# A fused two-layer decoder: norms without an aggregate instruction, a feed gate by silu, and rounding and a maximum moved to ScalarE

## The chip, the cores and the metric

The kernel runs on one core of a Trainium2 chip. A core has five engines with an instruction queue each: TensorE (PE, matrix products), VectorE (DVE), ScalarE (ACT, activation functions), GpSimd (POOL), and SyncE (SP), which here only issues DMA transfers. Each engine works through its queue in order, and semaphores make one wait for another. The metric is the device time of one execution in microseconds, the median of several.

## What is computed

The reference sends 64 sequences of 128 tokens with 128 features through two layers. After each of the six blocks x becomes layernorm(x + block(x)). The blocks of layer 0 are an attention by running exp(k)-weighted means, a cross-attention with 16 heads over 77 context rows with bias and mask, and a feed of two shared and eight routed experts, two for each token. Those of layer 1 are a selective state-space scan (256 channels, 16 states), a cross-attention with 16 heads of 64 that ends in a norm of its own, and a quantised feed.

```python
def _layernorm(x, axis=-1, eps=1e-05):
    m = jnp.mean(x, axis=axis, keepdims=True)
    v = jnp.var(x, axis=axis, keepdims=True)
    return (x - m) / jnp.sqrt(v + eps)
...
    gate = jax.nn.silu(_bitlinear(x, w_gate))
    up = _bitlinear(x, w_up)
    return _bitlinear(gate * up, w_down)
```

In the scan block delta = softplus(dt @ W + bias); the state is h = exp(delta * A) * h + (delta * u) * B per step, and y = sum over the states of h * C. In the quantised feed the activations are rounded to 127 steps of each row's largest magnitude and the weights to -1, 0 and 1.

## The kernel before

Everything stays on the core between blocks, except that x of each group goes through DRAM (`mid`) and that rows are sorted by expert in DRAM (`rows_in`, `rows_out`). The 64 sequences are cut into 16 groups of 4 (128 partitions of tokens, 4 x 128 features). In layer 0 a group passes a (attention), b (cross-attention) and c (routing, shared experts); each two groups make a chunk `ch`, whose tokens are sent by indirect DMA from GpSimd (L977) into 15 tiles of 256 rows (`c_tile`, L317 to L390), multiplied by the tile's expert and gathered again (`c_get`, L392 to L426). Four chunks are done beside layer 0 and four beside layer 1. In layer 1 a group passes the scan (`scan_inputs`, `spread`, `decays`, `states`, `outputs`), cross-attention and feed.

The order of the work is made when the kernel is built. Each block is a generator that yields steps: an engine, a cost written by hand in microseconds, a key, the keys it waits for, a function that issues its instructions, and buffers from fixed lists of slots. `Flow.run` picks again and again the step that can start first by these costs, so the cost of a step, the table that it names (`exp`, `silu`, `ln`; a change of table counts 1.3) and the flag `port` (steps of VectorE and GpSimd with it are not laid over each other) decide where its instructions stand in each engine's queue. On the chip, the queues are fixed and waits are by semaphore.

The steps that the change and the prediction name:

- `norm` (L255 to L279): for each of 4 sequences VectorE takes statistics (bn_stats, L261: a row is split in two halves, each giving count, mean and summed squared deviation) and joins them (bn_aggr, L262); GpSimd adds epsilon, takes the power -0.5 and the shift (L269 to L272); ScalarE applies both (L278). It is called 16 times each for lnA, lnB and lnC (after the three blocks of layer 0), and ln1, ln2, ln3 and ln4 in layer 1; 8 of the lnC calls lie in layer 1.
- The scan: 16 pairs of states per group. Per pair VectorE makes bu = du * B (L1375) and the scan h (L1383); ScalarE the decays dA (L1359, three buffers, table `exp`); GpSimd h * C (L1407); TensorE adds up over states (L1420). The product h * C also waits for the bu of the following pair, which is issued ahead of the following scan.
- Softplus of delta (L1268 to L1299): abs on ScalarE (L1278), maximum with 0 on VectorE (L1282), then exponential and logarithm on ScalarE.
- The feed (L1702 to L1808): for each of 4 sequences TensorE makes gate and up, ScalarE tanh (L1758, same table as exp), VectorE the gate product g = (tanh + 1) * gate (L1762), times up (L1766), the row's maximum and four or five small scales (L1772, L1696 to L1699, L1774), the first half of rounding by adding a large number (L1777); ScalarE takes the number off again (L1783).
- In `c_get`, GpSimd issues two gathers per sequence (L417) and VectorE adds each, weighted, to v (L406, two instructions per sequence).
- Mask addition of cross-attention in layer 0 on GpSimd (L684), with three bias buffers and one mask buffer.

```python
            (got,) = yield S.flow.pool(2.0, k + ("got", b), out, get, S.got, landing=3.0)
            got.until = k + ("mix", b)
            yield Fork(mix(b, got))
```

Of the kernel before, what the change touches and what calls it, by code (L numbers as in the profile page):

```python
# [11 lines left out]
AF = mybir.ActivationFunctionType  # L12
ALU = mybir.AluOpType
# [4 lines left out]
P = 128  # L18
B = 64
G = 4  # L20
NG = B // G
W = G * P
M = 77
# [3 lines left out]
MAGIC = 12582912.0  # L27
RMS_EPS = 1.1920929e-07
LN_EPS = 1e-5
# [39 lines left out]
class Flow:  # L69
# [18 lines left out]
    pe, act, dve, pool = _maker("PE"), _maker("ACT"), _maker("DVE"), _maker("POOL")  # L88
# [92 lines left out]
def decoder(ctx: ExitStack, tc: tile.TileContext, t: dict, out: bass.AP):  # L181
# [30 lines left out]
    pool.memset(mhalf, -0.5)  # L212
    mmagic = new(const, [P, 1], "mmagic")
    pool.memset(mmagic, -MAGIC)
    before = new(const, [P, NE, NE], "before")
    pool.memset(before, 1.0)
    pool.affine_select(
# [37 lines left out]
    def norm(flow, pn, key, o, v, deps):  # L255

        kind = key[0]
        mv, st = new(pn, [P, G, 2], kind + "mv"), new(pn, [P, G, 6], kind + "st")

        def stats(b):  # L260
            dve.bn_stats(st[:, b, :], v[:, b, :])  # L261
            dve.bn_aggr(mv[:, b, :], st[:, b, :])  # L262

        for b in range(G):
            yield flow.dve(0.55, key + ("st", b), deps, lambda: stats(b))
        r, sh = new(pn, [P, G], kind + "r"), new(pn, [P, G], kind + "sh")

        def steps():
            pool.tensor_scalar(r, mv[:, :, 1], LN_EPS, None, ALU.add)  # L269
            pool.tensor_scalar(sh, mv[:, :, 0], -1.0, None, ALU.mult)  # L270
            pool.tensor_tensor(r, r, mhalf[:, :G], ALU.pow)
            pool.tensor_tensor(sh, sh, r, ALU.mult)  # L272

        yield flow.pool(2.0, key + ("r",), [key + ("st", b) for b in range(G)], steps)
        for b in range(G):
            yield flow.act(
                0.5, key + (b,), [key + ("r",)],
                lambda: act(o[:, b, :], v[:, b, :], AF.Identity, bias=sh[:, b : b + 1], scale=r[:, b : b + 1]),  # L278
            )  # L279
# [112 lines left out]
    def c_get(g, S):  # L392

        k, ch = ("c", g), g // CH
        out = [("tile", ch, i, "out") for i in range(NT)]
        yield Wait(out + [("sum", g)])
        (vs,) = yield S.flow.sp(k + ("v",), [("sum", g)], lambda o: nc.sync.dma_start(out=o, in_=mid[g]), S.v)
        vs.until = ("out0", g)
        v = vs.tile

        def mix(b, got):
            j = g % CH * G + b

            def add():
                for i in range(2):
                    dve.scalar_tensor_tensor(  # L406
                        v[:, b, :], got.tile[:, i, :], gate[:, ch, i, j : j + 1], v[:, b, :], ALU.mult, ALU.add
                    )

            yield S.flow.dve(0.7, k + ("mix", b), [k + ("got", b), k + ("v",)], add)  # L410

        for b in range(G):

            def get(o):
                j = g % CH * G + b
                for i in range(2):
                    pool.indirect_dma_start(  # L417
                        out=o[:, i, :], out_offset=None, in_=rows_out[ch],
                        in_offset=bass.IndirectOffsetOnAxis(ap=pos[:, ch, i, j : j + 1], axis=0),
                    )  # L420

            (got,) = yield S.flow.pool(2.0, k + ("got", b), out, get, S.got, landing=3.0)
            got.until = k + ("mix", b)
            yield Fork(mix(b, got))
        yield from norm(S.flow, S.pn, ("lnC", g), v, v, [k + ("mix", b) for b in range(G)])
        yield S.flow.sp(("out0", g), normed(("lnC", g)), lambda: nc.sync.dma_start(out=mid[g], in_=v))  # L426

# [13 lines left out]
    with (  # L441
# [17 lines left out]
        sl_wkv = slots(4, p, [P, 2, P], "wkv")  # L459
        sl_den = slots(3, p, [P, P], "den")  # L460
        sl_y = slots(3, p, [P, G, P], "y")
        sl_ah = slots(1, p, [P, W], "ah")
        sl_v = slots(3, p, [P, G, P], "v")
        sl_bias = slots(3, p, [P, G, M], "bias")
        sl_mask = slots(1, p, [P, G, M], "mask")
        sl_cg = slots(3, p, [P, G * M], "cg")
        sl_xb = slots(2, p, [P, G, P], "xb")
        sl_qT = slots(3, p, [P, W], "qT")
        sl_kb = slots(2, p, [P, G, 4, M], "kb")
        sl_s = slots(4, p, [P, NH, M], "s")  # L470
# [5 lines left out]
        sl_eh = slots(2, p, [P, 2, W], "eh")  # L476
        sl_sum = slots(2, p, [P, G, P], "sum")
        sl_pick = slots(2, p, [P, 2, NE, CH * G], "pick")
        S = Experts(flow=flow, bank=bank, pn=pn, a=sl_a, ahead=-0.5, pace=lambda ch, i: [], **tile_slots(p, 2, 2, 2, 2, 2, 1, 3))
        zero = new(p, [P, P], "zero")  # L480
        pool.memset(zero, 0.0)

# [15 lines left out]
        scale = 8**-0.5  # L498
# [470 lines left out]
        def c_send(ch):  # L969
            yield Wait([("rank", ch), ("fill", ch)])  # L970
            for g, b, i in (key[1:] for key in sent(ch)):

                def send():
                    j = g % CH * G + b
                    if len(filled[ch]) > 1:
                        pool.memset(tick, 0.0)
                    one = pool.indirect_dma_start(  # L977
                        out=rows_in[ch], in_=CX[g, "x"][:, b, :], in_offset=None,
                        out_offset=bass.IndirectOffsetOnAxis(ap=pos[:, ch, i, j : j + 1], axis=0),
                    )  # L980
# [8 lines left out]
                yield POOL(1.0, ("send", g, b, i), [("rank", ch), ("fill", ch), ("c", g, "x")], send, landing=3.0)  # L989

        def c_shared(g):
            k = ("c", g)
# [80 lines left out]
    with (  # L1073
# [131 lines left out]
        def scan_inputs(g):  # L1205
# [61 lines left out]
            for c in range(2):  # L1267
                step = lambda z, *_: mm(  # L1268
                    z, dt_proj[:, c * P : (c + 1) * P], proj.tile[0:NS, :], start=True, stop=True
                )  # L1270
                if c == 0:
                    pz, e, delta, du = yield PE(0.95, k + ("dt", c), [k + ("proj",)], step, bank, sl_h, sl_delta, sl_du)
                else:
                    (pz,) = yield PE(0.95, k + ("dt", c), [], step, bank)
                pz.until = k + ("max", c)
                bias = dt_bias[:, c : c + 1]
                yield ACT(
                    0.7, k + ("abs", c), [k + ("dt", c)], lambda: act(e.tile[:, c, :], pz.tile, AF.Abs, bias=bias)  # L1278
                )
# [422 lines left out]
        def feed(g):  # L1702
# [6 lines left out]
            def quantise():  # L1709
                dve.tensor_reduce(am, x, AX.X, ALU.max, apply_absolute_value=True)  # L1710
                xs, xi = scales(am, G)
                dve.tensor_scalar(sg, xi, wmean[:, 0:1], 0.5, ALU.mult, ALU.mult)
                dve.tensor_scalar(su, xi, wmean[:, 1:2], None, ALU.mult)
                dve.tensor_tensor(su, su, sg, ALU.mult)
                q["xs"] = xs

            yield DVE(2.0, k + ("am",), normed(("ln3", g)), quantise)
# [26 lines left out]
            for b in range(G):  # L1744

                def gate_up(pg, pu, _):
# [29 lines left out]
                def scaled():  # L1776
                    dve.tensor_scalar(h, h, w["hs"], MAGIC, ALU.mult, ALU.add)  # L1777
# [152 lines left out]
```

## Time and profile before

| what | value |
|---|---|
| median of 3 executions | 3314.45 us (3307.13 to 3314.62) |
| the profiled execution: its time, its span | 3323.51 us, 3321.7 us |
| instructions | 55836 |
| TensorE matmul busy | 2867.3 us, 86% of the span |
| VectorE busy | 2616.4 us, 79% |
| ScalarE busy | 2097.9 us, 63% |
| GpSimd busy | 1741.2 us, 52% |
| mean granted TensorE clock | 0.941 |
| first, last scan (L1383) on VectorE | about 1117, 3187 us from the start |

The span runs from the first to the last instruction; the execution's time has 1.8 us more around it. A group of the profile is a line, an engine, an operation and its tiles, then busy time and mean nanoseconds of one, then the idle time just before these instructions and what ended it. "A <- B" in the list of waits says that A's engine stood idle until B was done. The list counts an engine's idle time, which is not the same as time lost at the end; for that there is the chain that ended last, which is followed back from the last instruction and here reaches over the last 1001 us. An operation of VectorE can last longer than its own work when GpSimd works at the same time: of the weighted sums L406 the shortest is 253 ns, the median 351, the longest 5274.

### The profile page before, as it was taken

Reading aid. Unit: us, or ns where it says so; the run is one execution under the profiler, and the core shown is the slowest. Engines: PE = TensorE matmul, PEld = TensorE weight load, DVE = VectorE, ACT = ScalarE, POOL = GpSimd, SP = SyncE. Lnnn points to the kernel's source line nnn. Section 1 sums busy time; section 2 is a strip of 40 time slices with the busy share of each in tenths; the row PEclk is TensorE's granted clock in tenths of the full one; section 3 lists DMA queues with packets and bytes.
Section 4 is the critical chain, followed back from the end, with each engine's and each line's share of the span. In section 5 each row is a group of like instructions: output and inputs, shape, how many; then the busy total and the mean of one; then the engine's idle time right before and its main releaser. Section 6 shows DMA issues by size and latency. Waiting matters only on the chain. (4 is left out here: it accounts for less than half of the span.)

```text
span 3321.7 us, 55836 instructions
## 1 busy us (share of the span) xinstructions
PE 2867.3 (86%) x19880; PEld 1937.7 (58%) x19880; DVE 2616.4 (79%) x5007; ACT 2097.9 (63%) x3831; POOL 1741.2 (52%) x1603
## 2 busy tenths in 40 slices
PE   3989999999996679889898988888899988888883
PEld 2667777776864346556464655555665655656462
DVE  3777787888754488878987888888888898879864
ACT  1655767667731566767666766666677767767653
POOL 3454564655454356445745556664645556554531
PEclk7899999999998899999998999999999999999986
DMA  5134252333223464365545554464536533333400
GB/s 152 46 95 123 71 142 71 108 105 85 67 82 117 140 232 151 128 189 172 188 149 179 178 180 166 147 213 154 173 118 196 173 119 127 116 121 122 154 23 7
DMA packets 256542, 438.23 MB, mean 132 GB/s; under 512 B 40683, under 2 KB 155014, under 8 KB 256262
## 3 DMA queue, kind: packets, MB, share of 16 engines
q1 hardware_dynamic: 248070, 417.86, 39.9%
q0 software_dynamic: 8192, 16.79, 1.6%
q8 instruction: 157, 2.57, 0.3%
q14 instruction: 123, 1.01, 0.1%
HBM read 376.37 MB, written 58.20 MB: 131 GB/s over the span
## 5 line engine op out<-in xcount | busy, mean ns | idle before, releaser
L1407 POOL TENSOR_TENSOR h<-h,C 128x1024 f32<-128x1024 f32 x256 | 604.6, 2363 | 571.4 <-DVE bu L1375 365.5
L1420 PE MATMUL acc<-h,ident 128*128 128x512 f32 x1024 | 540.1, 653 | 138.5 <-POOL h L1407 137.5
L1383 DVE TENSOR_TENSOR_SCAN h<-dA,bu 128x1024 f32<-128x1024 f32 x256 | 583.8, 2280 | 26.7 <-PE acc L1420 7.7
L1375 DVE TENSOR_TENSOR bu<-du,B 128x1024 f32<-128x1024 f32 x256 | 355.8, 1390 | 79.2 <-DMA B<-rows 77.2
L1420 PEld LDWEIGHTS acc<-h,ident 128*128 128x128 f32 x1024 | 187.2, 201 | 346.5 <-POOL h L1407 193.5
L1359 ACT ACTIVATE dA<-delta,negA 128x508 f32<-128x508 f32 x512 | 336.4, 714 | 57.2 <-DVE h L1383 56.7
L349 PE MATMUL mm<-t_rT,t_we 128*128 128x256 f32 x960 | 250.8, 394 | 14.9 <-DMA t_we<-in_we 6.7
L1609 POOL TENSOR_TENSOR s<-s,rs 128x1232 f32<-128x1232 f32 x64 | 145.6, 2276 | 175.7 <-DVE rs L1603 111.6
L349 PEld LDWEIGHTS mm<-t_rT,t_we 128*128 128x128 f32 x960 | 175.9, 194 | 76.5 <-issue 22.6
L785 POOL TENSOR_TENSOR s<-s,mx 128x1232 f32<-128x1232 f32 x64 | 144.0, 2255 | 143.9 <-DVE mx L782 69.5
L1509 PE MATMUL mm<-xT,w_yWq 128*128 128x256 f32 x512 | 165.6, 406 | 21.4 <-ACT kT L1502 8.9
L1627 ACT COPY pT<-mm 77x512 f32<-77x512 f32 x256 | 136.4, 583 | 55.9 <-PE mm L1616 53.9
L1498 ACT ACTIVATE qT<-mm,w_ybq 128x256 f32<-128x256 f32 x256 | 122.4, 478 | 68.7 <-PE mm L1510 67.8
L793 ACT COPY pT<-mm 77x512 f32<-77x512 f32 x256 | 132.7, 586 | 50.8 <-PE mm L800 45.1
L1566 PEld LDWEIGHTS mm<-kT,qT 64*128 64x128 f32 x2048 | 130.3, 194 | 51.3 <-issue 18.6
L1616 PE MATMUL mm<-ident,s 128*77 128x128 f32 x1024 | 140.9, 283 | 19.7 <-POOL s L1609 10.6
L977 POOL DMA_INDIRECT rows_in<-cx,pos x128 | 124.3, 971 | 57.9 <-DVE pos L957 24.9
L800 PE MATMUL mm<-ident,s 128*77 128x128 f32 x1024 | 139.3, 290 | 17.1 <-ACT s L787 12.4
L417 POOL DMA_INDIRECT t_got<-rows_out,pos x128 | 131.2, 1025 | 40.6 <-issue 28.5
L1616 PEld LDWEIGHTS mm<-ident,s 128*77 128x77 f32 x1024 | 118.9, 152 | 54.8 <-POOL s L1609 21.8
L1566 PE MATMUL mm<-kT,qT 64*128 64x77 f32 x2048 | 148.0, 286 | 0.9 <-DVE s L1592 0.4
L374 PEld LDWEIGHTS mm<-t_we,t_th 128*128 128x128 f32 x960 | 123.6, 197 | 32.8 <-issue 15.1
(335 smaller groups left out, 7025.5 us busy)
## 6 DMA issues: line engine op xcount, KB each, us to landing
B<-rows SPq DMA_DIRECT2D x256, 512.0 KB, 4.9
C<-rows SPq DMA_DIRECT2D x256, 512.0 KB, 4.0
t_we<-in_we SPq DMA_DIRECT2D x120, 384.0 KB, 3.6
rows_in<-zero SPq DMA_DIRECT2D x8, 1920.0 KB
t_row<-rows_in SPq DMA_DIRECT2D x120, 128.0 KB, 3.2
rows_out<-t_yo SPq DMA_DIRECT2D x120, 128.0 KB, 3.6
cg<-in_ctxT SPq DMA_DIRECT2D x32, 154.0 KB, 4.4
x<-in_x SPq DMA_DIRECT2D x16, 256.0 KB, 4.2
```

The source lines that it names most:

```text
L349: mm(o[:, c * TR : (c + 1) * TR], we.tile[:, n * 256 + c * P : n * 256 + (c + 1) * P], rT.tile, start=True, stop=True,)
L785: lambda: pool.tensor_tensor(s, s, mx.tile.unsqueeze(2).to_broadcast([P, NH, M]), ALU.subtract), port=True,
L800: nc.tensor.transpose(pt[0:M, i * P : (i + 1) * P], s[:, 4 * q + i, :], ident)
L1359: act(dA[:, j, :, 1:], delta[:, c, :, 1:], AF.Exp, scale=negA[:, c, n + j : n + j + 1])
L1375: order[g, c, n] = dve.tensor_tensor(bu, du[:, c, :].unsqueeze(1).to_broadcast([P, 2, W]), BC["B", g, c, n], ALU.mult)
L1383: dve.tensor_tensor_scan(h.rearrange("p n s -> p (n s)"), DA[g, c, n].rearrange("p n b s -> p (n b s)"), bu.tile.rearrange("p n s -> p (n ...
L1407: one = pool.tensor_tensor(h, h, BC["C", g, c, n], ALU.mult)
L1420: mm(acc, ident, HS[g, c, n][:, j, :], start=n + j == 0, stop=n + j == NS - 1)
L1509: mm(pk[:, 0 : 2 * P], yWq[:, cs], xT.tile[:, pair * 2 * P : (pair + 1) * 2 * P], start=True, stop=True)
L1566: mm(sc[:, i * M : (i + 1) * M], qT[r, i, b2 * P : (b2 + 1) * P], kT[r, i, b2 * M : (b2 + 1) * M], start=True, stop=True,)
L1609: lambda: pool.tensor_tensor(s, s, rs.tile.unsqueeze(2).to_broadcast([P, NH, M]), ALU.mult), port=True,
L1616: nc.tensor.transpose(pt[0:M, i * P : (i + 1) * P], s[:, 4 * q + i, :], ident)
```

## The change

Seven edits:

1. `norm` drops bn_aggr. GpSimd joins the two halves itself: d is the difference of the means, r the sum of the squared deviations over 128 plus epsilon plus d squared over 4, sh minus half the sum of the means. Ten instructions of GpSimd where there were four.
2. In the feed, ScalarE's silu (table `silu`) takes the place of tanh and VectorE's gate product; one small multiplication of scales goes too.
3. The first half of rounding moves from VectorE to ScalarE (scale and a bias tile `magic`).
4. Delta's maximum with 0 moves from VectorE to ScalarE (Relu with the same bias).
5. The weighted sum of an even sequence waits for the gathers of the odd one behind it as well.
6. Gathers and sends carry the flag `port`.
7. Slots in layer 0: `ah` 1 to 2, `bias` 3 to 2, `xb` 2 to 3, and the expert tiles' row buffer 2 to 1.

```diff
+    magic = new(const, [P, 1], "magic")
+    pool.memset(magic, MAGIC)
...
-        def stats(b):
-            dve.bn_stats(st[:, b, :], v[:, b, :])
-            dve.bn_aggr(mv[:, b, :], st[:, b, :])
...
-            yield flow.dve(0.55, key + ("st", b), deps, lambda: stats(b))
+            yield flow.dve(0.3, key + ("st", b), deps, lambda: dve.bn_stats(st[:, b, :], v[:, b, :]))
...
-            pool.tensor_scalar(r, mv[:, :, 1], LN_EPS, None, ALU.add)
-            pool.tensor_scalar(sh, mv[:, :, 0], -1.0, None, ALU.mult)
+            pool.tensor_tensor(d, st[:, :, 1], st[:, :, 4], ALU.subtract)
+            pool.tensor_tensor(r, st[:, :, 2], st[:, :, 5], ALU.add)
+            pool.tensor_tensor(sh, st[:, :, 1], st[:, :, 4], ALU.add)
+            pool.tensor_tensor(d, d, d, ALU.mult)
+            pool.tensor_scalar(r, r, 1.0 / P, LN_EPS, ALU.mult, ALU.add)
+            pool.tensor_scalar(d, d, 0.25, None, ALU.mult)
+            pool.tensor_scalar(sh, sh, -0.5, None, ALU.mult)
+            pool.tensor_tensor(r, r, d, ALU.add)
             pool.tensor_tensor(r, r, mhalf[:, :G], ALU.pow)
             pool.tensor_tensor(sh, sh, r, ALU.mult)
-        yield flow.pool(2.0, key + ("r",), [key + ("st", b) for b in range(G)], steps)
+        yield flow.pool(3.3, key + ("r",), [key + ("st", b) for b in range(G)], steps)
...
-            yield S.flow.dve(0.7, k + ("mix", b), [k + ("got", b), k + ("v",)], add)
+            yield S.flow.dve(0.7, k + ("mix", b), [k + ("got", b | 1), k + ("v",)], add)
...
-            (got,) = yield S.flow.pool(2.0, k + ("got", b), out, get, S.got, landing=3.0)
+            (got,) = yield S.flow.pool(2.0, k + ("got", b), out, get, S.got, landing=3.0, port=True)
...
-        sl_ah = slots(1, p, [P, W], "ah")
+        sl_ah = slots(2, p, [P, W], "ah")
-        sl_bias = slots(3, p, [P, G, M], "bias")
+        sl_bias = slots(2, p, [P, G, M], "bias")
-        sl_xb = slots(2, p, [P, G, P], "xb")
+        sl_xb = slots(3, p, [P, G, P], "xb")
...
-        S = Experts(flow=flow, bank=bank, pn=pn, a=sl_a, ahead=-0.5, pace=lambda ch, i: [], **tile_slots(p, 2, 2, 2, 2, 2, 1, 3))
+        S = Experts(flow=flow, bank=bank, pn=pn, a=sl_a, ahead=-0.5, pace=lambda ch, i: [], **tile_slots(p, 2, 1, 2, 2, 2, 1, 3))
...
-                yield DVE(
-                    0.75, k + ("max", c), [k + ("dt", c), k + ("abs", c)],
-                    lambda: dve.tensor_scalar(delta.tile[:, c, :], pz.tile, bias, 0.0, ALU.add, ALU.max),
+                yield ACT(
+                    0.7, k + ("max", c), [], lambda: act(delta.tile[:, c, :], pz.tile, AF.Relu, bias=bias)
                 )
...
-                    0.7, k + ("tanh", b), [k + ("up", b)],
-                    lambda: act(h, pg.tile, AF.Tanh, scale=sg[:, b : b + 1]), table="exp",
+                    0.7, k + ("g", b), [k + ("up", b)],
+                    lambda: act(h, pg.tile, AF.Silu, scale=sg[:, b : b + 1]), table="silu",
                 )
                 yield DVE(
-                    0.7, k + ("g", b), [k + ("tanh", b)],
-                    lambda: dve.scalar_tensor_tensor(h, h, 1.0, pg.tile, ALU.add, ALU.mult),
-                )
-                yield DVE(
-                    0.75, k + ("h", b), [],
+                    0.75, k + ("h", b), [k + ("g", b)],
                     lambda: dve.scalar_tensor_tensor(h, pu.tile, su[:, b : b + 1], h, ALU.mult, ALU.mult),
...
-                yield DVE(0.45, k + ("scaled", b), [], scaled, port=True)
+                yield ACT(
+                    0.75, k + ("scaled", b), [k + ("scale", b)],
+                    lambda: act(h, h, AF.Identity, scale=w["hs"], bias=magic),
+                )
```

The send of L989 carries the flag like the gather. In the built order, the counts per engine are the same on TensorE and SyncE; VectorE has 624 fewer instructions, GpSimd 673 more, ScalarE 96 more and 26 more table loads.

More of the change, by code (lines that the diff above doesn't have):

```diff
@@ L257, in norm @@
         kind = key[0]
-        mv, st = new(pn, [P, G, 2], kind + "mv"), new(pn, [P, G, 6], kind + "st")
-        def stats(b):
-            dve.bn_stats(st[:, b, :], v[:, b, :])
-            dve.bn_aggr(mv[:, b, :], st[:, b, :])
+        st = new(pn, [P, G, 6], kind + "st")
         for b in range(G):
-            yield flow.dve(0.55, key + ("st", b), deps, lambda: stats(b))
-        r, sh = new(pn, [P, G], kind + "r"), new(pn, [P, G], kind + "sh")
+            yield flow.dve(0.3, key + ("st", b), deps, lambda: dve.bn_stats(st[:, b, :], v[:, b, :]))
+        r, sh, d = new(pn, [P, G], kind + "r"), new(pn, [P, G], kind + "sh"), new(pn, [P, G], kind + "d")
         def steps():
-            pool.tensor_scalar(r, mv[:, :, 1], LN_EPS, None, ALU.add)
-            pool.tensor_scalar(sh, mv[:, :, 0], -1.0, None, ALU.mult)
+            pool.tensor_tensor(d, st[:, :, 1], st[:, :, 4], ALU.subtract)
[6 more added lines that the diff above has]
+            pool.tensor_tensor(r, r, d, ALU.add)
             pool.tensor_tensor(r, r, mhalf[:, :G], ALU.pow)
             pool.tensor_tensor(sh, sh, r, ALU.mult)
-        yield flow.pool(2.0, key + ("r",), [key + ("st", b) for b in range(G)], steps)
+        yield flow.pool(3.3, key + ("r",), [key + ("st", b) for b in range(G)], steps)
         for b in range(G):
@@ L987, in send @@
                     filled[ch].append(one)
-                yield POOL(1.0, ("send", g, b, i), [("rank", ch), ("fill", ch), ("c", g, "x")], send, landing=3.0)
+                yield POOL(1.0, ("send", g, b, i), [("rank", ch), ("fill", ch), ("c", g, "x")], send, landing=3.0, port=True)
         def c_shared(g):
@@ L1711, in quantise @@
                 xs, xi = scales(am, G)
-                dve.tensor_scalar(sg, xi, wmean[:, 0:1], 0.5, ALU.mult, ALU.mult)
+                dve.tensor_scalar(sg, xi, wmean[:, 0:1], None, ALU.mult)
                 dve.tensor_scalar(su, xi, wmean[:, 1:2], None, ALU.mult)
-                dve.tensor_tensor(su, su, sg, ALU.mult)
                 q["xs"] = xs
@@ L1774, in scale @@
                     dve.tensor_scalar(w["hi"], w["hi"], wmean[:, 2:3], None, ALU.mult)
-                def scaled():
-                    dve.tensor_scalar(h, h, w["hs"], MAGIC, ALU.mult, ALU.add)
                 yield DVE(1.2, k + ("scale", b), [], scale)
-                yield DVE(0.45, k + ("scaled", b), [], scaled, port=True)
+                yield ACT(
+                    0.75, k + ("scaled", b), [k + ("scale", b)],
+                    lambda: act(h, h, AF.Identity, scale=w["hs"], bias=magic),
+                )
                 (hb,) = yield ACT(
```

## The prediction

> **What bounds the kernel now.** I read the page's engine shares first, then busy time cut into stages, then the waits, then the chain that ended last. The shares of the page are means over a program with two halves, so the stages come before any of them is believed. Columns: microseconds, then busy time with instruction counts of TensorE matmul, TensorE weight load, VectorE, ScalarE and GpSimd, granted clock, DMA share, GB/s.
>
> ```profile
> 0.00:200.00 200.00, 134.38 (x1038) 91.25 (x1038) 127.27 (x379) 81.16 (x170) 77.45 (x135) 0.85 0.35 100
> 200.00:1000.00 800.00, 765.43 (x7419) 584.76 (x7417) 616.49 (x1628) 518.35 (x1017) 433.64 (x598) 0.98 0.34 95
> 1000.00:1117.00 117.00, 79.75 (x321) 46.26 (x321) 44.45 (x131) 33.36 (x48) 44.25 (x75) 0.84 0.30 99
> 1117.00:3187.00 2070.00, 1808.66 (x10477) 1156.99 (x10478) 1759.22 (x2660) 1401.58 (x2471) 1156.52 (x758) 0.95 0.49 160
> 3187.00:3321.70 134.70, 79.11 (x630) 58.44 (x628) 68.92 (x210) 63.44 (x127) 29.33 (x39) 0.76 0.02 5
> ```
>
> Row two is layer 0 in full flow: TensorE is busy 765/800 = 96%, VectorE 77%. TensorE bounds it, and VectorE work taken out there gives nothing. Row four is layer 1 with its scans, 62% of the span: TensorE 87%, VectorE 85%, ScalarE 68%, GpSimd 56%. No engine is full; two in-order queues near 86% wait for each other. Which waits:
>
> ```profile
> POOL h L1407 <- DVE bu L1375: 365.5, 110, 13.6
> PEld acc L1420 <- POOL h L1407: 193.5, 142, 7.0
> PEld acc L1420 <- issue: 148.9, 545, 0.8
> PE acc L1420 <- POOL h L1407: 137.5, 107, 6.2
> ```
>
> The largest wait of TensorE, 137.5 of about 261 idle us in row four, is for the product h*C on GpSimd, and that product waits 365.5 us for the next bu in VectorE's queue. So what stands ahead of a bu in VectorE's queue sets when TensorE gets its accumulation. The chain agrees:
>
> ```profile
> PE 13%; DVE 9%; POOL 3%; ACT 2%; issue 2%; DMA 1%; SPq 0%; POOLq 0%; DVEq 0%; ACTq 0%
> L1383 DVE TENSOR_TENSOR_SCAN h<-dA,bu 128x1024 f32<-128x1024 f32 x256 | 583.8, 2280 | 26.7 <-PE acc L1420 7.7
> L1375 DVE TENSOR_TENSOR bu<-du,B 128x1024 f32<-128x1024 f32 x256 | 355.8, 1390 | 79.2 <-DMA B<-rows 77.2
> L1359 ACT ACTIVATE dA<-delta,negA 128x508 f32<-128x508 f32 x512 | 336.4, 714 | 57.2 <-DVE h L1383 56.7
> ```
>
> The chain reaches back over the last 1001 us only; of those TensorE has 416, VectorE 312, GpSimd 107, ScalarE 74. The scan's idle time names no ScalarE decay, and the decays wait 56.7 us for scans instead: ScalarE runs ahead.
>
> **VectorE, what goes.** Durations of the trace, where visible as distance from start to start. Aggregates: statistics plus aggregate take 0.40 us, four short L1722 operations in a row 0.21 each, so 0.19 per aggregate (at least the 0.10 between an aggregate and its successor). In row four lie 260 of the 448: 49 us; 160 lie in layer 0 (30 us, behind a full TensorE), 28 in the tail. Gate product L1762: 0.79 us, 56 in row four, 44 us. Rounding L1777: 0.41 between, 56, 23 us. Delta's maximum L1282: 0.67, 30, 20 us; its wait for ScalarE (21.5 us in this stage) goes too, but what was behind it is next, so I count none. Small scales: 14 at 0.2, 3 us. Sum 139 of 1759 us.
>
> **ScalarE, what comes.** Silu takes the place of tanh at the same length (L1758, 683 ns). Maximum: like its neighbour abs L1278, 685 ns, 32 times, 22 us. Rounding with a scale and a bias: like L1783, 720 ns, 64 times, 46 us. Both may be up to 0.1 us longer or shorter each, 10 us. Table loads: the built order of the changed kernel has 172 in layer 1 against 142, and 44 against 48 in layer 0. A load takes 1283 ns in the trace: 30 x 1.283 = 38 us, together 106 us. Here the Trainium skill speaks against the change: "ScalarE: Activation LUTs", section What ACT_TABLE_LOAD costs, adds a drain of about 1.38 us to the 1283 ns, 2.66 us per switch. By that the loads would be 80 us, the sum 148. The trace shows at one of them:
>
> ```profile
> 2105.14 0.58 ACT L1258 COPY fh<-mm 48x512 f32<-48x512 f32 x1 [2.06 <-PE mm L1253]
> 2105.73 1.28 ACT L1599 ACT_TABLE_LOAD   x1
> 2107.03 1.23 ACT L1599 ACTIVATE s<-s 128x1232 f32<-128x1232 f32 x1
> ```
>
> Copy, load and exponential follow without a gap, so no drain is paid and I take 106 (1402 to about 1500 of row four, 75% of a shortened stage). 34 of the loads stand before the feed's silu and 47, six more, before decays: silu and exp now alternate within the feed. A decay behind such a pair is 2.6 us later. What hides it is the decays' lead over the scans; without the lead, a scan, the bu behind it and TensorE's accumulation wait.
>
> **GpSimd, what comes.** A norm gets eight short steps where it had two, and keeps power and product. Neighbours of the same size: L531 and L532, 0.20 us, L533 0.23, spaced 0.28 to 0.31. Six more at 0.20 to 0.29: 1.2 to 1.75 us, I take 1.6. 72 norms in layer 1: 115 us; 112 in all: 180 us. Row four rises from 56% to about 62%. The skill's "GPSIMD Engine Reference", section Engine selection, would keep elementwise work on VectorE as about twice as fast; at 128x4 the rows say 0.20 to 0.23 against 0.15 to 0.23 on VectorE (L1696 to L1714), because nearly all is fixed cost. By the rule the steps would cost VectorE half, by the rows as much. What the change buys is not speed but another queue: a norm is later by 1.6 - 4 x 0.19 = 0.8 us. Behind it in GpSimd's queue stand h*C and the softmax products L1609; they idle 747 us in all, so most of it is covered. Uncovered, the 65 norms of row four by 1.6 us: 104 us.
>
> **Pairs of transfers, slots, order.** The sums L406 take 253 ns at least, but 82.3/128 = 643 on average: 50 us are stretched beside GpSimd operations (5.7 us for two of them while h*C and softmax products ran). In the built order the two blocks of a pair follow each other, so a sum waits for one transfer more (up to 32 pairs x 2 x 0.97 us of issuing = 62 us, with a scan or an attention step behind it) or escapes some stretch and the 9.6 us of waiting seen (up to -60). I take zero: both gathers are usually issued together. The new port flags only shift order. In layer 0 the second tile row buffer goes: a row lands in 3.2 us while 60 tiles spread over some 700 us, one per 11; between 0 and +10 us, I take zero, as TensorE is full there. The opening stall stays: GpSimd's second mask addition waits 33 us for a mask queued behind two zero fills, and in the built order it still does. The tail keeps its length: per block VectorE gives up 0.79 + 0.41, ScalarE adds 0.72, two norms add 0.8 each: about -2 + 2.
>
> **The sum.** From below: a microsecond of work counts as far as its engine's work is on the chain. Cut to the chain's last 1001 us, busy time is 813 us on VectorE, 657 on ScalarE, 506 on GpSimd; so 312/813 = 0.38, 74/657 = 0.11, 107/506 = 0.21. Gain 139 x 0.38 = 53; costs 100 x 0.11 = 11 (row four's part of the 106) and 104 x 0.21 = 22; net -20 us. From above: if TensorE came as close to full in row four as in row two (96%), 1809/0.957 = 1890, -180 us. The first is too low, as it leaves out that with VectorE at 79% two queues no longer catch on each other; the second too high, as 149 us of TensorE's gaps are issue gaps at the accumulation that no VectorE time fills. Between these I take TensorE at 90%: 1809/0.90 = 2010, -60 us. The choice of 90 is mine: a third of the way, since TensorE's row two level needed VectorE at 77%, and VectorE here comes to 1620/2010 = 81%. The profiled execution took 3323.5 us (span 3321.7 and 1.8 around it), 9 above the median; less 60 it is 3263.5, and against the median 3314.5 - 60 = 3255 us.
>
> **Rivals.** *Layer 1 fills as layer 0 does*: row two shows that this program's mix can keep TensorE at 96%. Against it speak the accumulation's issue gaps. -100 to -180, some 3180 us. *TensorE holds the end anyway*: its chain share is the largest, no matmul is removed, and the -20 of the marginal sum melts with the uncovered costs: 3304 to 3324. *ScalarE becomes the bound, slower*: place, the decays behind the feed's silu in row four. All 106 us of ScalarE's added time surface if ScalarE's lead of three decay buffers is gone, against the 60 gained: +46, 3360; with a third of the gain left, up to 3380. It decides from about 60 us of the 106 on. For it: 75% in an in-order queue that also empties five PSUM banks. Against it: scans waiting for no decay, and ScalarE's 7% of the chain. *The change doesn't relieve VectorE*: excluded, 139 us are gone from its queue; only what follows is open.
>
> **How the numbers follow.** Partial relief, 3255, own range 3200 to 3304: 0.53. Full relief below 3200: 0.17. No change, within 0.3% (about 10 us, what a measurement of this kernel can tell from no change): 0.09. Slower: 0.21, of it half below 3340. The range 3165 to 3340 leaves out about 0.06 below and 0.10 above. Faster by over 0.3%: 0.70; within: 0.09; slower: 0.21.
>
> **What would show it.** VectorE's busy time down by about 170 us in all, ScalarE's up by about 100, GpSimd's by 130 to 180. Accumulation's wait for h*C (137.5) and h*C's for bu (365.5) shrink, TensorE's share between first and last scan is 90%, and layer 0's full stage stays near 96%. The slower rival shows as scans idle before ScalarE decays. I am wrong if VectorE's freed time comes back as waits for norms, table loads or banks.

## The result, and the profile after

| | before | after |
|---|---|---|
| median of four executions | 3311.89 us (3307.13 to 3314.62) | 3394.22 us (3387.50 to 3411.86) |
| ratio, 95% interval | | 1.0254 [1.0227, 1.0282] |
| profiled execution: time, span | 3323.51, 3321.7 | 3387.50, 3385.5 |
| VectorE, ScalarE, GpSimd busy | 2616.4, 2097.9, 1741.2 | 2478.6, 2203.2, 1867.8 |
| start of first scan; first to last scan start; from there to the end | 1119; 2056; 146 | 1111; 2125; 150 |

The changed kernel is slower by 82 us; 3255 was forecast, 60 faster. A second set of runs of it gave 1.0246 [1.0206, 1.0286]. The profiled spans differ by 64 us: -8 before the first scan, +68 in the scan stage, +3 behind it. So nearly all lies in the stage that the change was to shorten. The last scan of the kernel before starts at 3175 us; the 3187 given further up, where its row four ends, is 12 us later.

Busy time cut into the same five stages, after (columns as in the prediction):

```profile
0.00:200.00 200.00, 136.19 (x1096) 91.15 (x1096) 136.67 (x399) 83.67 (x174) 90.84 (x183) 0.91 0.35 101
200.00:1000.00 800.00, 757.03 (x7387) 575.31 (x7388) 599.32 (x1486) 513.18 (x1011) 470.48 (x804) 0.99 0.34 95
1000.00:1111.00 111.00, 76.02 (x293) 44.49 (x292) 34.08 (x93) 35.70 (x52) 36.49 (x62) 0.81 0.31 102
1111.00:3238.00 2127.00, 1821.34 (x10491) 1170.49 (x10510) 1651.62 (x2240) 1496.33 (x2578) 1226.44 (x1136) 0.94 0.47 155
3238.00:3385.50 147.50, 79.43 (x594) 57.97 (x596) 56.96 (x169) 74.29 (x140) 43.55 (x94) 0.75 0.02 6
```

Counted in both from the first to the last scan's start, VectorE gave up 106 us (1755 to 1649), and its idle time rose by 174 (301 to 475). TensorE works 22 us longer there (1797 to 1819) and stands idle 46 us longer (259 to 305); its share fell from 87% to 86%. No engine became full: the busiest is still TensorE, and ScalarE and GpSimd stand at 70% and 58%. The waits of the whole run:

```profile
POOL h L1410 <- DVE bu L1378: 359.4, 114, 10.5
PEld acc L1423 <- POOL h L1410: 207.9, 144, 7.7
PE acc L1423 <- POOL h L1410: 152.5, 111, 7.5
PEld acc L1423 <- issue: 149.1, 542, 0.8
```

The wait for bu is where it was (365.5 to 359.4), although VectorE has 106 us less to do in that stage: the queue in front of bu didn't get emptier in a way that reaches the accumulation. TensorE's wait for h*C rose from 137.5 to 152.5, and within the stage its wait for the other products on GpSimd, those of the softmax, rose as well (before, then after):

```profile
PE mm L1616 <- POOL s L1609: 10.6, 9, 3.7
PE mm L1619 <- POOL s L1612: 26.5, 12, 11.9
```

These two make 31 of TensorE's 46 us of added idle time. The chain that ended last, and the three groups that the prediction showed of before:

```profile
PE 36%; DVE 18%; POOL 11%; DMA 7%; ACT 6%; issue 4%; SPq 1%; POOLq 0%; DVEq 0%; ACTq 0%
L1386 DVE TENSOR_TENSOR_SCAN h<-dA,bu 128x1024 f32<-128x1024 f32 x256 | 584.4, 2283 | 67.6 <-ACT dA L1362 22.7
L1378 DVE TENSOR_TENSOR bu<-du,B 128x1024 f32<-128x1024 f32 x256 | 365.8, 1429 | 86.3 <-DMA B<-rows 83.9
L1362 ACT ACTIVATE dA<-delta,negA 128x508 f32<-128x508 f32 x512 | 334.3, 714 | 46.6 <-DVE h L1386 45.9
```

This time the chain goes back over most of the run, so its shares can't be set beside those of before. The scan's idle time rose from 26.7 to 67.6 us, and its first releaser is now a decay on ScalarE: the sign named for the slower rival, with 22.7 us, not with 60. What VectorE waits for within the scan stage, largest first (total, times, longest), then two of these lines before:

```profile
DVE bu L1378 <- DMA B<-rows: 83.9, 53, 4.3
DVE mx L1591 <- PE mm L1569: 47.4, 20, 7.7
DVE xb L1675 <- PE mm L1668: 42.6, 19, 9.9
DVE u L1434 <- PE acc L1423: 40.2, 20, 6.8
DVE x L1802 <- PE mm L1796: 27.9, 14, 4.8
DVE fh L1763 <- ACT fh L1759: 25.0, 14, 5.3
```

```profile
DVE mx L1588 <- PE mm L1566: 20.3, 17, 5.8
DVE fh L1762 <- ACT fh L1758: 2.5, 4, 1.0
```

Of the others, bu stood at 77.2 before, xb at 35.0, u at 24.4 and x at 7.2. The new idle time has no single place: softmax maximum, out-projection, end of scan and feed all wait longer for TensorE, and the feed's up product for silu. No one wait accounts for the stage.

### The profile page after: what moved, and what is told of

Same layout as the page of the kernel before. It is cut to its first block, busy times and chain, and to the rows that moved or that the text cites. A ratio compares the mean times of both kernels' runs of the same rounds, so it can differ in the third digit from the quotient of the medians.

```text
span 3385.5 us, 55789 instructions
## 1 busy us (share of the span) xinstructions
PE 2870.0 (85%) x19859; PEld 1939.4 (57%) x19880; DVE 2478.6 (73%) x4383; ACT 2203.2 (65%) x3953; POOL 1867.8 (55%) x2276
## 4 chain that ended last, share of the span: by engine, by line
PE 36%; DVE 18%; POOL 11%; DMA 7%; ACT 6%; issue 4%; SPq 1%; POOLq 0%; DVEq 0%; ACTq 0%
PE acc L1423 7%; POOL h L1410 6%; DMA B<-rows 5%; DVE bu L1378 3%; DVE h L1386 3%; PE mm L1234 3%; PE mm L353 3%; PE mm L1639 2%; PE mm L1619 2%; PE mm L1668 2%; PE mm L1533 2%; PE mm L1569 2%; DVE mx L1591 2%; PE mm L378 1%; DVE s L1595 1%
## 5 line engine op out<-in xcount | busy, mean ns | idle before, releaser
L1410 POOL TENSOR_TENSOR h<-h,C 128x1024 f32<-128x1024 f32 x256 | 607.1, 2373 | 568.6 <-DVE bu L1378 359.4
L1423 PE MATMUL acc<-h,ident 128*128 128x512 f32 x1024 | 550.8, 664 | 153.3 <-POOL h L1410 152.5
L1386 DVE TENSOR_TENSOR_SCAN h<-dA,bu 128x1024 f32<-128x1024 f32 x256 | 584.4, 2283 | 67.6 <-ACT dA L1362 22.7
L1378 DVE TENSOR_TENSOR bu<-du,B 128x1024 f32<-128x1024 f32 x256 | 365.8, 1429 | 86.3 <-DMA B<-rows 83.9
L1591 DVE TENSOR_REDUCE mx<-mm 128x4 f32<-128x308 f32 x256 | 119.4, 466 | 53.5 <-PE mm L1569 52.4
```

Source lines behind the costliest of these rows:

```text
L1378: order[g, c, n] = dve.tensor_tensor(bu, du[:, c, :].unsqueeze(1).to_broadcast([P, 2, W]), BC["B", g, c, n], ALU.mult)
L1386: dve.tensor_tensor_scan(h.rearrange("p n s -> p (n s)"), DA[g, c, n].rearrange("p n b s -> p (n b s)"), bu.tile.rearrange("p n s -> p (n ...
L1410: one = pool.tensor_tensor(h, h, BC["C", g, c, n], ALU.mult)
L1423: mm(acc, ident, HS[g, c, n][:, j, :], start=n + j == 0, stop=n + j == NS - 1)
L1591: lambda: dve.tensor_reduce(mx.tile[:, h4], sc4, AX.X, ALU.max),
```

## The experiments

The runs were on two kinds of chips: on some the kernel before takes 3422 to 3431 us, on others 3311.5 to 3314.7. On the slower kind the part before the first scan is 96 to 149 us longer, while the scan stage came out alike for the changed kernel's order, which ran on both (2114 and 2126 there, with parts of its work put back, 2118 and 2125 here). No program was profiled on both kinds, so it is likely, and not shown, that the stage doesn't depend on the chip. Ratios are always against the kernel before on the same chip; "stage" is the time from the first to the last scan's start.

**The arithmetic of the norms alone, order of before.** The new instructions with the planner's old costs:

```diff
-            dve.bn_aggr(mv[:, b, :], st[:, b, :])
...
-            yield flow.dve(0.55, key + ("st", b), deps, lambda: stats(b))
+            yield flow.dve(0.55, key + ("st", b), deps, lambda: dve.bn_stats(st[:, b, :], v[:, b, :]))
```

GpSimd's ten steps are those of the change, still planned at 2.0.

> The kernel before with the norm's new instructions but its old costs, so that every other instruction keeps its place in its queue. If the new steps themselves cost (GpSimd's 10 in place of 4, about 1.6 us later per norm, at 104 us of GpSimd work in the scan stage), this run is slower by 20 us or more. If they are covered and the loss of the whole change comes from order or from other parts, it lies within 10 us of the kernel before, or up to 30 us faster by the 79 us taken off VectorE.

Measured: 1.0116 [1.0090, 1.0142]; first scan 1223, stage 2086. It is a cost, and no gain shows.

**The planner's costs alone**, old instructions, 0.3 and 3.3 in place of 0.55 and 2.0: nothing but the order moves.

> The opposite: the norm's old instructions, laid out by its new costs (0.3 in place of 0.55 for statistics, 3.3 in place of 2.0 for GpSimd). No work changes, only the order. If the order is what lost time, this run is slower by 20 us or more; if only work matters, it lies within 10 us of the kernel before.

Measured: 1.0079 [1.0057, 1.0101]; first scan 1241, stage 2052.6. An order alone costs 0.8%, ahead of the first scan (the order of before starts scanning at 1223 to 1235 on this kind of chip).

**Silu alone** (edit 2), with its planned table:

> Only the feed's gate by silu: 64 gate products of VectorE gone, the table changes between silu and exp come. If table changes are the cause (ScalarE's loads in front of decays and gates), this part alone is slower by 30 us or more, with scans idle before decays and the product after the gate idle before silu. If VectorE's time counts, it is faster by 20 us; if order alone rules, it may fall on either side of that by about 30.

Measured: 1.0009 [0.9994, 1.0023], stage 2037.8. The page counts 238 table loads against 190, and 0.79 us of VectorE per block less: together nothing, in an order that was drawn anew.

**Another order of the kernel before.** The planner lets an engine see another's result after `LAG`; a change of it reorders, and nothing else:

```diff
-    LAG = 0.15
+    LAG = 0.16
```

> A control: the kernel before with the wait between engines taken as 0.16 in place of 0.15 when the order is made. Nothing is added or removed, the order alone shifts everywhere. If the scatter of orders is a cause of the size of the loss, this run differs from the kernel before by 20 us or more in either direction; if the order is harmless, by less than 10.

Measured: 1.0211 [1.0189, 1.0233]; first scan 1287, stage 2062. So a neighbour of the old order, with the same instructions, costs almost as much as the whole change, though elsewhere: ahead of the first scan, and not in the stage. From here on two things had to be told apart: what the new work costs, and what the order that was drawn costs.

**Rounding alone** (edit 3), **maximum alone** (edit 4), and **edits 5 to 7 alone**, which change no arithmetic. Each draws its own order, so work and order are not told apart here:

> Only the first half of rounding on ScalarE. If ScalarE's added 46 us surface behind the row maxima, slower by 20 us or more; if VectorE's freed 23 us count, faster by up to 20; if only order decides, within about 30 on either side.

Measured: 1.0080 [1.0049, 1.0111], stage 2071.6.

> Only delta's maximum on ScalarE: 32 instructions change engine, 22 us. Work alone would move the time by less than 10 us either way; a larger move would be the order's.

Measured: 1.0013 [1.0001, 1.0025], stage 2061.3.

> Only the edits that change no arithmetic: sums that wait for pairs of gathers, port flags, and the slots of layer 0. If these lose time, slower by 20 us or more, seen as later tiles and a later first scan in layer 0 (one row buffer) or as sums that wait for gathers; if not, within 10 us.

Measured: 1.0247 [1.0220, 1.0273]. Pairs, port flags and slots, which the prediction took at zero, cost by themselves what all seven edits cost, but most of it in another place: the first scan starts at 1177 instead of 1119, where the changed kernel starts at 1111, and the stage takes 2090. The two signs named for work in these edits did not come. The sums' waits for gathers and TensorE's waits for rows, first before, then here:

```profile
DVE t_v L406 <- DMA t_got<-rows_out,pos: 9.6, 9, 3.6
PE mm L339 <- DMA t_row<-rows_in: 14.9, 3, 11.3
```

```profile
DVE t_v L406 <- DMA t_got<-rows_out,pos: 9.0, 10, 2.4
PE mm L339 <- DMA t_row<-rows_in: 15.0, 2, 11.4
```

So neither the pairing nor the missing row buffer shows as a wait of its own, which leaves the arrangement; none of the three edits ran alone. The end of layer 0 and the scan stage in its profile, then TensorE's time line in the former (start, length, in brackets the idle time ahead and its releaser):

```profile
1000.00:1177.00 177.00, 108.83 (x681) 64.40 (x672) 60.48 (x157) 58.67 (x92) 40.02 (x56) 0.73 0.19 61
1177.00:3267.00 2090.00, 1819.46 (x10526) 1164.19 (x10526) 1782.50 (x2674) 1413.90 (x2479) 1156.35 (x766) 0.95 0.48 158
```

```profile
1064.26 0.80 PE L832 MATMUL mm<-w_xWo,oT 128*128 128x128 f32 x2 [1.44 <-DVE oT L828]
1075.23 1.11 PE L518 MATMUL mm<-ident,cx 128*128 128x128 f32 x4 [10.17 <-DMA cx<-mid]
...
1121.62 0.76 PE L1116 MATMUL acc<-hb,ones 1*128 1x128 f32 x2 [26.93 <-DMA w_yWv<-in_yWv]
```

In front of the transposes L518 TensorE stands for 10.2 us with nothing to do but wait for the last block's rows; before, all such waits came to 2.5 us. In front of L1116, for weights of layer 1, it stands for 26.9 us, before for 20.8. What could fill such time are the first products of the shared experts (L1000). Of their 256 in the trace, 140 are left behind the last softmax transposes of layer 0 (L800) in the kernel before, 96 in the changed one, 16 here. Orders with 140 start scanning at 1117 to 1127 us, with 96 at 1111 to 1116, with 72 at 1136, with 16 at 1177; on the slower chips at 1223 to 1235 with 140, 1259 with 96, and 1230 to 1287 with 16 to 32. So they go with the start of the scans roughly, and don't fix it alone.

**Other orders of both kernels**, `LAG` 0.16 in the changed one, then 0.14 and 0.17 in both:

> A control: the changed kernel laid out with a wait between engines of 0.16 in place of 0.15. All its work stays. If the changed kernel's loss of 2.5% is that of its work, this one also lies at +2 to +3%; if the loss is mostly that of one order among many, it may lie 1% or more away from the changed kernel, on either side.

> A control of order: the kernel before laid out with a wait between engines of 0.14. If the kernel before owes its time to one good order among many, this one is slower by 0.5 to 2.5%, as with 0.16; if 0.16 was a single bad draw, it lies within 0.3%.

> The same with 0.17; again 0.5 to 2.5% slower if the order of the kernel before is a good draw, within 0.3% if not.

> The changed kernel laid out with 0.14. If the changed kernel's own order is a bad draw, this one lies below it, at 0 to +1.5% against the kernel before; if its work costs 2.5%, it stays at +2 to +3%. If the changed work were a gain hidden by order, some of these draws would fall below the kernel before.

> The changed kernel laid out with 0.17; the same readings as with 0.14. The mean of the four orders of each kernel is compared: equal means within 0.5% say that the change's work is neutral and that its own order lost; a mean 1% or more above says that the work costs.

Measured, with lag16_before and the two kernels themselves beside them (stage in us):

| LAG | before: ratio, stage | changed: ratio, stage |
|---|---|---|
| 0.14 | 1.0161 [1.0126, 1.0196], 2073.5 | 1.0194 [1.0160, 1.0228], 2078.1 |
| 0.15 | 1, 2056.4 | 1.0254 [1.0227, 1.0282], 2124.8 |
| 0.16 | 1.0211 [1.0189, 1.0233], 2062.1 | 1.0078 [1.0055, 1.0102], 2038.9 |
| 0.17 | 1.0187 [1.0155, 1.0218], 2096.8 | 1.0102 [1.0062, 1.0143], 2058.8 |
| mean | 1.014, 2072 | 1.0157, 2075 |

This table answers most of it. Over four orders the two kernels differ by 0.2% in time and 3 us in the stage; between orders of one kernel the stage scatters with a standard deviation of 18 us (before) and 37 us (changed), so the 3 us carry a standard error of some 20. (LAG 0.15 and the changed kernel's 0.16 ran on the quicker kind of chip, the others on the slower; on the quicker kind alone, the changed kernel's two orders stand 86 us of stage apart.) In time, the order of before is the best of its four by 1.6%; that of the changed kernel is the worst of its four. Without these two, the three other orders put the changed kernel's stage 19 us below that of before (2059 against 2077, standard error some 15), so even the sign of the work is open; a gain of 60 lies well outside either way. The stage of the changed kernel in its best order:

```profile
1136.00:3175.00 2039.00, 1775.77 (x10294) 1129.44 (x10294) 1617.98 (x2209) 1478.60 (x2552) 1228.24 (x1133) 0.95 0.50 162
```

The same kinds of work as in row four above, 88 us shorter. About half of that is work that moved: 197 matmuls, 46 us of TensorE, lie outside the stage in this order, and the parts in front of it and behind it are 25 and 10 us longer. The whole span is 51 us shorter.

**Relief of VectorE by itself, order of before.** First the aggregates go, then the gate product and the first half of rounding as well; ScalarE and GpSimd get nothing new:

```diff
-            dve.bn_aggr(mv[:, b, :], st[:, b, :])
...
-            pool.tensor_scalar(r, mv[:, :, 1], LN_EPS, None, ALU.add)
-            pool.tensor_scalar(sh, mv[:, :, 0], -1.0, None, ALU.mult)
+            pool.tensor_scalar(r, st[:, :, 2], LN_EPS, None, ALU.add)
+            pool.tensor_scalar(sh, st[:, :, 1], -1.0, None, ALU.mult)
```

> The kernel before, in its own order, with the 448 aggregates left out: the norms take mean and variance of one half of each row, with GpSimd's four steps as before. 85 us less VectorE work, nothing added. By the prediction's rate of 0.38 the scan stage's part (49 us) gives -19 us, by a full TensorE more; if VectorE's time is worth nothing at a given order, within 10 us. With norm_work at +1.2%, the difference is the price of GpSimd's six extra steps.

> The same, and also the feed's gate product and the first half of rounding left out (the gate is only the hyperbolic tangent, and the feed's values are not rounded): about 160 us less VectorE work in the run, some 115 of it in the scan stage, nothing added and every other instruction at its old place. The prediction's rate gives -44 us, TensorE at 90% of the stage -60, a full TensorE -150; if VectorE's time is worth nothing without a new order, within 10 us.

Measured: 0.9934 [0.9912, 0.9955], stage 2035.3; and 0.9836 [0.9814, 0.9859], stage 2020.3. The stage's row of the latter:

```profile
1235.00:3255.00 2020.00, 1781.72 (x10409) 1143.28 (x10424) 1655.27 (x2283) 1392.89 (x2464) 1149.12 (x755) 0.96 0.50 163
```

VectorE at 1655 us, as in the changed kernel, and TensorE at 88%. Taking 1755 - 1655.5 = 99 us off VectorE shortens the stage by 36: 0.36 us per us. The rate is rough: the aggregates give 21 us for 42, the other two 15 for 57, and a stage repeats within some 6 us. Behind the last scan another 22 us go (146 to 124).

The two kernels without aggregates differ in the work of GpSimd's norms alone, ten steps against four: 1.0116 against 0.9934, and a stage of 2086 against 2035:

```profile
1223.00:3309.00 2086.00, 1810.04 (x10420) 1153.29 (x10422) 1719.77 (x2396) 1398.03 (x2464) 1223.42 (x1145) 0.95 0.49 158
1228.00:3263.00 2035.00, 1782.29 (x10398) 1145.41 (x10412) 1712.48 (x2395) 1396.68 (x2462) 1144.10 (x755) 0.96 0.49 162
```

Two waits rise with them, ScalarE's for a norm's shift and TensorE's for h*C. First with ten steps, then with four:

```profile
ACT x L280 <- POOL ln3sh L274: 40.7, 14, 9.6
ACT x L280 <- POOL ln1sh L274: 35.8, 14, 7.5
ACT xb L280 <- POOL ln2sh L274: 22.8, 11, 5.2
PE acc L1422 <- POOL h L1409: 143.4, 111, 5.2
```

```profile
ACT x L277 <- POOL ln1sh L271: 21.1, 6, 5.8
ACT x L277 <- POOL ln3sh L271: 20.4, 7, 7.8
ACT xb L277 <- POOL ln2sh L271: 12.7, 7, 4.1
PE acc L1419 <- POOL h L1406: 125.5, 101, 5.9
```

ScalarE waits 45 us longer for these shifts, and TensorE 18 us longer for h*C, which stands in the same queue as the norms; that is most of the 23 us by which TensorE's idle time in the stage rises. Which of the two ways costs the 51 us isn't shown.

**The changed kernel's own order, with single parts of its work put back**: old norm instructions under the new costs, and the function Tanh in Silu's place, so that the feed lacks its gate product:

> The changed kernel in its own order with the norm's old instructions (aggregates on VectorE, four steps on GpSimd). If the norm's new steps cost here what they cost in the order of before (1.2%), this run lies at about +1.3% against the kernel before; if the changed kernel's loss is its order's, it stays at +2 to +3%.

> The changed kernel in its own order with the gate's silu replaced by the hyperbolic tangent, which needs no table change (the gate is then another function): 31 table loads fewer, 40 us of ScalarE. If table changes are on the path, this run is 30 us or more below the changed kernel, at +1.5% or less against the kernel before; if they are covered, it stays at +2.5%.

Measured: 1.0240 [1.0217, 1.0262], stage 2114.4; and 1.0293 [1.0261, 1.0325], stage 2125.6, with 185 table loads in place of 216. The stage's rows:

```profile
1259.00:3373.00 2114.00, 1820.55 (x10470) 1172.06 (x10490) 1675.12 (x2494) 1497.06 (x2577) 1147.27 (x751) 0.94 0.48 156
```

```profile
1260.00:3385.00 2125.00, 1824.03 (x10470) 1172.35 (x10490) 1644.78 (x2238) 1460.39 (x2550) 1224.93 (x1135) 0.94 0.47 155
```

GpSimd is relieved by 79 us in one and ScalarE by 36 in the other, and the stage stays at 2114 and 2125. The first is an exchange, as the aggregates come back to VectorE (1675 us against 1652), so it tests the edit of the norms as a whole. In this order neither that edit nor silu's loads cost the stage more than some 10 us; the order, the maximum and the rounding are left, and the other orders of the changed kernel, with the same maximum and rounding, take 2039 to 2078.

**The changed kernel once more, and silu's table loads in the order of before**: silu stands where tanh stood, its loads unknown to the planner, and the gate product, which silu contains, goes:

> The changed kernel once more, beside the kernel before on the same chip. If table changes are covered, it lies within 0.4% of the +2.9% of the kernel with the hyperbolic tangent; if they cost their 40 us, at +4%. If the norm's new steps cost at this order as at the order of before, it lies 1.2% above the +2.4% of the kernel with the old norm.

> The kernel before in its own order, with silu in the place of tanh and the gate product left out, as the change has it, but laid out as if silu needed no table of its own: 89 table loads more, 114 us of ScalarE, and 64 gate products of VectorE fewer. If ScalarE's loads are covered, the run gains the gate's 51 us times 0.36, about -18 us; if they surface, it is slower by 30 us or more, with scans idle before decays.

Measured: 1.0246 [1.0206, 1.0286], stage 2118.4, so the stage of one order repeats within some 6 us. The ratio lies 0.5% below the kernel with the hyperbolic tangent and 0.1% above the one with the old norm, so neither cost shows, with the reserve that those two ran on the slower kind of chip. The other run: 1.0079 [1.0048, 1.0109], stage 2075. The loads rose from 190 to 279, and those at decays from 41 to 72. The group and the stage's row:

```profile
L1359 ACT ACT_TABLE_LOAD x72 | 92.4, 1283 | 4.8 <-DVE h L1383 3.7
```

```profile
1127.00:3202.00 2075.00, 1800.86 (x10397) 1154.57 (x10411) 1729.81 (x2586) 1497.65 (x2542) 1149.87 (x755) 0.95 0.49 159
```

The stage is 19 us longer than before, where the missing gate product by itself should give 44 x 0.36 = 16 back: about 35 of 80 x 1.283 = 103 us of loads in the stage come through, 0.3 per us, by this estimate. The sign named, scans idle before decays, didn't come; it is the feed's up product that now waits for silu, 24.5 us in the run.

## Why the prediction was wrong

- **What goes from VectorE and what comes elsewhere: right in kind, VectorE's saving somewhat short.** VectorE lost 138 us in all where 170 were forecast, in the stage 106 for 139 (10 of the difference is the bu, which grew from 1390 to 1429 ns each), ScalarE gained 105 (106 reckoned in layer 1 alone), GpSimd 127 (130 to 180). Layer 0's full stage stayed at 757/800 = 95%, and the tail at +3 (0 forecast). Table loads were paid without a drain: in the changed kernel's trace the median load starts 17 ns behind the operation ahead of it and is followed after 12 ns. The rule cited for GpSimd was read too widely: the Trainium skill's "GPSIMD Engine Reference", section Engine selection, says twice as slow of operations with two inputs, and three of the eight steps have one. Nothing in the sum rested on it.
- **The failed step: "Pairs of transfers, slots, order. [...] I take zero", with "The new port flags only shift order".** Order is not zero: edits 5 to 7 together cost +2.5%, with no longer waits for rows or gathers; the flags alone weren't run. The prediction counted each moved instruction and took the arrangement of the others as given. But edits, costs and slots make the planner draw a new order of all 55 thousand instructions. Four other orders of the kernel before with nothing else changed (three by `LAG`, one by the planner's costs) were all slower, by 0.8% to 2.1%; silu alone and maximum alone, which draw anew too, stayed within 0.2%, so not every draw loses. Of the 128 us by which the stage missed the forecast (2125 instead of 2056 - 60), the table of orders gives 50 to the changed kernel's own draw (2125 against its mean of 2075) and 16 to that of before (2056 against 2072); the rest is the next step. These are means of four draws, so each share is good to some 20 us.
- **The other half: the work is worth about 0, not -60.** Means of 2075 and 2072, give or take 20. Three terms of the sum were mis-sized.
  "Between these I take TensorE at 90%": with VectorE relieved as forecast and no new cost, TensorE reached 88% and the rate was 0.36, not the 60/139 = 0.43 net of all costs that I chose. The estimate "from below" had used 0.38, close to it; layer 0's 96% was no guide to this stage. The reason given against the upper estimate was misread as well: the 149 us of issue gaps at the accumulation are those of the weight loads (PEld), which overlap matmuls. TensorE's matmuls waited in row four for other engines and DMA alone, 137.5 us of it for h*C.
  "Uncovered [...] 104", of which I took 22: in the order of before the six steps cost 51 us of the stage. Mis-sized by more than a factor of two, within the bound. Their length wasn't the reason, being shorter than I took (below).
  "100 x 0.11 = 11" for ScalarE: silu's loads came through at about 0.3 per us, which would make it about 30 if the rest of ScalarE's new work counts alike (an estimate; that rest wasn't run at a held order). With these sizes the sum from below is -139 x 0.36 + 51 + 30 = about +30 in the order of before. In the changed kernel's own order the norms' edit and the loads cost 10 us or less; in that of before the norms' edit as a whole cost 30. So the price of the same work depends on the order that it stands in.
- **The slower rival.** Its sign came, scans waiting for decays by 22.7 us, but it isn't the cause: 31 fewer table loads in the same order left the stage and this wait (24.4 us) where they were, while the three other orders of the changed kernel, with all of its ScalarE work, have 7 to 11 us of it. "TensorE holds the end anyway" was the nearest to what the work does. The order as a mechanism of its own was not among the rivals, and should have been the one on the slower side.
- **"I am wrong if VectorE's freed time comes back as waits for norms, table loads or banks."** It came back as waits, +174 us in the stage. By the releaser named, VectorE waits 117 us longer for TensorE and 59 us longer for ScalarE, while TensorE itself waits longer mainly for GpSimd (148 to 178 us), whose load had grown.

Left open: which part of the changed kernel's order costs the 50 us of its stage. The norms' edit and the table loads are excluded; maximum, rounding and pairs were not taken out at that order. The counts of shared-expert products go with the start of the scans, and were not set by themselves. No version that computes all of the reference and beats the kernel before was found; further draws of the order weren't tried.

## What to carry to other kernels

Where a planner makes a static order for all engines, an edit is two changes: its work, and a new draw of the order. Measure the scatter of draws first, by a knob that leaves every instruction as it is; here it was 2%, more than the work that was priced at a held order (the norms' edit 1.2%, silu's 0.8%), and an order that is the best among its neighbours has more to lose than to gain from a new draw. A stage is a fair measure of two orders only with the work inside it counted. To price the work, hold the order (give the planner the old costs) and change the instructions, or take means over several orders of both kernels.

## What the runs showed of the hardware

GpSimd starts steps of 128x4 every 0.15 to 0.28 us, faster than the 0.28 to 0.31 that I had read off their neighbours. The last norm of the changed kernel, eight steps and then the power:

```profile
3377.25 0.20 POOL L267 TENSOR_TENSOR ln4d<-ln4st 128x4 f32<-128x4 f32 x1 [35.24 <-DVE ln4st L263]
3377.41 0.20 POOL L268 TENSOR_TENSOR ln4r<-ln4st 128x4 f32<-128x4 f32 x1
...
3378.92 1.04 POOL L275 TENSOR_TENSOR ln4r<-ln4r,mhalf 128x4 f32<-128x4 f32 x1
```

From the first step to the power 1.67 us, against 0.50 with two steps: +1.17 per norm, where 1.6 was taken. And 51 us of the stage still came of it, with longer waits for the norm on ScalarE and for h*C on TensorE.

The chips are not alike: in the order of before with few edits, the 800 us from 200 on had a granted clock of 0.98 on one kind and 0.93 to 0.94 on the other, with TensorE busy for 763 to 765 and 724 to 734 of them. With that go 96 to 116 us more before the first scan. In the scan stage the granted clock was 0.95 to 0.96 on both kinds, and no difference can be seen.
